# The first token tile's gate and up products spread over the last set of the cross attention

## The chip, the cores and the metric

The kernel runs on one core of one Trainium2 chip, as a single launch. The metric is device time in microseconds (us) of an execution. TensorE (PE, with its weight loads as PEld) does the matrix products, VectorE (DVE), ScalarE (ACT) and GpSimd (POOL) the elementwise work, and SyncE (SP) issues most of the DMAs.

## The reference

A pre-norm decoder layer in float32 over x of (4, 512, 512) tokens, with a context of (4, 1024, 512):

```python
x = x + _L0_attn_ref(_layernorm(x), ...)      # sliding-window self attention, grouped output
x = x + _L0_xattn_ref(_layernorm(x), ctx, ctx, mask, ...)   # 16 heads, 4 key groups, ALiBi
x = x + _L0_ffn_ref(_layernorm(x), w_gate, w_up, w_down)
```

The change touches the seam between the second and the third line. The cross attention is `softmax(Q K^T / sqrt(32) + slope * rel) V`, then a product with `Wo`. The feed-forward part quantizes its input per token to 8 bits and its weights to -1, 0, 1:

```python
gate = bitlinear(x, w_gate)                    # act_quant(x) @ weight_quant(w).T, 512 -> 2048
up = bitlinear(x, w_up)
intermediate = jax.nn.silu(gate) * up
return h_bitlinear(intermediate, w_down)       # Walsh-Hadamard transform over 2048, quantize, 2048 -> 512
```

## The kernel before

Three stages follow each other: the self attention, the cross attention, the feed-forward loop. The 2048 tokens are 16 token tiles of 128 rows.

**Cross attention.** The work is cut into `SETS` = 16 sets (4 batches times 4 heads of a group), and each set into 8 steps of 128 keys, 128 steps in all, 0 to 127. A step has, on TensorE in the order that is written in the code: row maxima of a set that lies ahead (L1085, 4 products into PSUM bank set "sm", each reduced by DVE, L1089), the score products (`scores`, L1145, two PSUM tiles `st` with two buffers), side work that a plan hangs on single steps (`extra`), the low-part products (`weights`, L1156), the exponentials on ACT (L1163, two of 128x1024 a step), and the weighted values of the step before (`weigh`, L1181). The exponentials are added up (L1170) by POOL, and in the last set by DVE, for the divisor (`divide`, L1195, copied by ACT at L1200). The row maxima run 10 steps ahead, so steps 118 to 127 have none. The last set is steps 120 to 127. Here only TensorE's order is fixed by hand; ACT, DVE and POOL are ordered by the scheduler.

**Tail of the cross attention.** After step 127: the last `weigh` and the last `divide`, four quotients (L1232, L1233) on DVE, the output products of the last two sets (`output`, L1240 on TensorE, added to the residual by DVE at L1245). Between them stand the gate and up products of the first token tile: `gated_mm(n)` makes 4 products for gate and 4 for up (L397, bf16, 128x512 each), then Silu on ACT (L402) out of PSUM; `gated_mul(n)` multiplies on DVE (L406); n is 0 to 3. `first(half)` is the first butterfly stage of the Walsh-Hadamard transform on DVE (L382, L383) from `mid` into `mix`.

**Feed-forward loop.** It runs s from 0 to 20 and works on five tiles at once: `now` is tile s, `prev` tile s-1, and so on. The order on TensorE, ACT and DVE is the written one. For `now`: `gated_mm`, `gated_mul`, `first`, and `turn(q)`, four transposes (L138) into one PSUM bank, copied by ACT (L139). For `prev`: the rest of the turns, `inner(q)`, four products with the 128x128 Hadamard matrix (L433), copied by ACT to `y` (L436), and the outer butterfly stages on DVE (`outer`, L382 and L383). For `old`: `sizes` (L445, absolute values on ACT), `peak` (L453 on DVE) and `quantize` (L326, L327 on ACT). Then the down product (L495). Two passes of the loop, s = 0 and s = 1, fill this pipe: at s = 0 only the first tile's `turn(0)` and `turn(1)` are done.

`mid` lies in the buffer "qs3" and `mix` in "qs2", one buffer each, both queries of cross-attention sets before. The gate weights are loaded at step 98 and the up weights at step 114. The rows of the tiles 12 and 13 are normalized in the loop (L92, L93 at s = 1).

Of the kernel before, what the change touches and what calls it, by code (L numbers as in the profile page):

```python
# [12 lines left out]
F32 = mybir.dt.float32  # L13
# [5 lines left out]
AF = mybir.ActivationFunctionType  # L19
ALU = mybir.AluOpType  # L20
# [3 lines left out]
P = 128  # L24
B, T, D = 4, 512, 512
NT = B * T // P
QT = T // P
DC = D // P
# [6 lines left out]
KT = KEYS // P  # L35
DH = 32
FF = 2048
FC = FF // P
# [15 lines left out]
def decoder_layer(  # L54
# [7 lines left out]
    nc = tc.nc  # L62
# [121 lines left out]
    def some_bank(shape, name):  # L184
        return bank["pool"].tile(shape, F32, tag=bank["tag"], name=name)
# [143 lines left out]
    xqTs, sgus = {}, {}  # L329
# [55 lines left out]
    class Tile:  # L385
# [23 lines left out]
            )  # L409

        def first(self, half):
            if half == 0:
                self.mix = bw.tile([P, FC, P], F32, tag="qs2", name="mix")
            butterfly(self.mid[:, ts(half, 8), :], self.mix[:, ts(half, 8), :], 0)
# [98 lines left out]
    with tc.tile_pool(name="aw", bufs=1) as aw, tc.tile_pool(name="akv", bufs=2) as akv, \  # L515
# [435 lines left out]
        with tc.manual_schedule(engines={mybir.EngineType.PE, mybir.EngineType.Activation}):  # L951
# [30 lines left out]
            for n in range(len(units) + 2):  # L982
                if n == len(units) - 3:
# [3 lines left out]
                    bx = late.enter_context(tc.tile_pool(name="bx", bufs=1, side="right"))  # L987
# [45 lines left out]
    bw = ctx.enter_context(tc.tile_pool(name="bw", bufs=1))  # L1033
    wT = {}

    def ternary_load(which):

        if which == "u":
            wT[which] = []
            for i in range(2):  # L1040
                w = bw.tile([P, DC // 2, FF], BF16, tag=f"qs{i}", name=f"w_u{i}")
                nc.sync.dma_start(out=w, in_=ternary[which][:, 2 * i:2 * i + 2, :])
                wT[which] += [w[:, 0], w[:, 1]]
        else:
            shape, tag = ([P, DC, FF], "ks0") if which == "g" else ([P, FC, D], "ks1")
            w = bw.tile(shape, BF16, tag=tag, name=f"w_{which}")
            for n in range(4):
                at = ts(n, shape[1] // 4)
                nc.sync.dma_start(out=w[:, at], in_=ternary[which][:, at])
            wT[which] = [w[:, c] for c in range(shape[1])]  # L1050

    with tc.tile_pool(name="b1", bufs=1) as b1, \
# [174 lines left out]
        def quotients(m):  # L1227
            nc.gpsimd.tensor_tensor(oTs[m], oTs[m], recs[m], ALU.mult)

        def quotient(m, qt):  # L1230
            rec, o = recs[m][:, ts(qt, P)], oTs[m][:, ts(qt, P)]
            nc.vector.reciprocal(rec, rec)  # L1232
            nc.vector.tensor_tensor(o, o, rec, ALU.mult)  # L1233
# [14 lines left out]


        SETS = B * HG  # L1250
        extra, at_end = {}, {}

        def plan(step, what, *args, to=extra):
            to.setdefault(step, []).append(lambda: what(*args))
# [82 lines left out]
                plan(step + 3 + i, side_rows, pair, to=at_end)  # L1337
        plan(KT * HG * 3 + 2, lambda: ternary_load("g"))
        plan(KT * HG * 3 + 18, lambda: ternary_load("u"))

        with tc.manual_schedule(engines={mybir.EngineType.PE}):
            nms[0] = small.tile([P, G, QT, 2], F32, tag="nm2", name="nm2", bufs=2)
            first.values(0)
            first.turn(2, nc.scalar)
            first.keys(2)
            first.values(1)
            first.turn(3)
            first.keys(3)  # L1350
            first.send(1)
            for i in range(G * QT):
                row_maxima(0, i)
                if i in (2, 4):
                    side_queries(1, i // 4)
                if i in (6, 8):
                    first.values(i // 2 - 1)
                if i == 8:
                    batches[1] = KeysValues(1)
                    batches[1].rows()  # L1360
            merge(0)
            last = None
            for step in range(-2, KT * SETS):
                m, kt = divmod(step, KT)
                now = 0 <= step < KT * SETS
                ahead, i0 = divmod(step + 10, KT)
                maxima = [
                    lambda i=i: row_max(ahead, 4 * i0 + i) for i in range(4)
                ] if 0 <= ahead < SETS else []
                for f in maxima[:2]:  # L1370
                    f()
                sts = [scores(m, kt, 0)] if now else None
                for f in maxima[2:3]:
                    f()
                if now:
                    sts.append(scores(m, kt, 1))
                for f in maxima[3:]:
                    f()
                for f in extra.pop(step, []):
                    f()  # L1380
                if maxima and i0 == KT - 1:
                    merge(ahead)
                ps = weights(m, kt, sts) if now else None
                if last is not None:
                    weigh(*divmod(step - 1, KT), last)
                if kt == 1 and 1 <= m < SETS:
                    divide(m - 1, before_last)
                    spread(m - 1)
                if kt == 2 and 1 <= m < SETS:
                    reciprocals(m - 1)  # L1390
                if kt == 4 and 1 <= m < SETS:
                    quotients(m - 1)
                for f in at_end.pop(step, []):
                    f()
                before_last, last = last, ps
            ternary_load("d")
            weigh(SETS - 1, KT - 1, last)
            divide(SETS - 1, last)
            scores_pool.close()
            gup = ctx.enter_context(tc.tile_pool(name="cgu", bufs=4, space=PSUM, side="right"))  # L1400
            tiles = [Tile(t) for t in range(NT)]
            tiles[0].gated_mm(0)
            tiles[0].gated_mm(1)
            for qt in range(QT):
                quotient(SETS - 1, qt)
            for n in range(2):
                tiles[0].gated_mul(n)
                tiles[0].gated_mm(n + 2)
                output(SETS - 2, (2 * n, 2 * n + 1), 2)
            for n in range(2, 4):  # L1410
                tiles[0].gated_mul(n)
            for half in range(2):
                tiles[0].first(half)
        assert not extra and not at_end
        late.close()


# [2 lines left out]
    with tc.tile_pool(name="c1", bufs=1) as c1, \  # L1420
            tc.tile_pool(name="c2", bufs=2) as c2, \
            tc.tile_pool(name="ctr", bufs=1, space=PSUM) as ctr, \
            tc.tile_pool(name="cdp", bufs=1, space=PSUM) as cdp, \
            tc.tile_pool(name="cmm", bufs=2, space=PSUM) as cmm, \
            tc.manual_schedule(
                engines={mybir.EngineType.PE, mybir.EngineType.DVE, mybir.EngineType.Activation}
            ):
        had = c1.tile([P, P], F32, name="had")
        nc.scalar.dma_start(out=had, in_=c_had)
        class Nothing:  # L1430
            def __getattr__(self, name):
                return lambda *args: None

        def tile_at(t):
            return tiles[t] if 0 <= t < NT else Nothing()

        last_xqT = c1.tile([P, QT, DC, P], BF16, name="xqT")
        last_rows = [
            ffn_rows(NT - 4 + i, 2, c1, ("h3", "xq"), (1, 1), lambda i0, i=i: last_xqT[:, i:i + 2])
            for i in (0, 2)  # L1440
        ]
        bank.update(pool=cmm, tag="mm")
        for s in range(NT + 5):
            now, prev, old, older, oldest = (tile_at(s - d) for d in range(5))
            if s == 0:
                now.turn(0)
                now.turn(1)
                continue
            older.back(0)
            old.sizes(0)  # L1450
            old.outer(3)
            if s <= NT:
                oldest.result()
            prev.inner(0)
            now.gated_mm(0)
            old.sizes(1)
            older.back(1)
            prev.inner(1)
            old.peak()
            if s > NT:  # L1460
                oldest.result()
            prev.turn(2)
            now.gated_mm(1)
            prev.turn(3)
            now.gated_mul(0)
            prev.inner(2)
            prev.inner(3)
            now.gated_mul(1)
            now.first(0)
            old.quantize(0)  # L1470
            if 1 <= s < 13:
                next(last_rows[(s - 1) // 6], None)
            now.gated_mm(2)
            now.turn(0)
            prev.outer(1)
            old.quantize(1)
            now.gated_mul(2)
            now.gated_mm(3)
            prev.outer(2)
            now.gated_mul(3)  # L1480
            now.first(1)
            older.down()
            now.turn(1)
# [53 lines left out]
```

## Time and profile before

| | us |
|---|---|
| median of 3 runs | 1608.52 |
| lowest, highest | 1608.39, 1610.01 |
| the profiled execution's own time | 1607.11 |
| its span | 1605.0 |
| TensorE busy in the span | 1553.0 |
| DVE busy | 1166.0 |
| ACT busy | 894.2 |
| POOL busy | 807.2 |

The profile is one execution of the program. Its span runs from the first to the last instruction; the execution's own time has 2.11 us more around it. A row of a timeline gives the start in the span, the time from the first instruction's start to the last one's end, the engine, the line of the code, the operation, output and inputs, and how many instructions were merged; in brackets stands the idle time of the engine before it and what released it. The end of a matmul is modelled, and matmuls overlap, so a run of four 128x512 products shows 1.03 us where the next run begins 0.865 us after it. A few matmul records are missing.

### The profile page before, as it was taken

Reading aid. Unit: us, or ns where it says so; the run is one execution under the profiler, and the core shown is the slowest. Engines: PE = TensorE matmul, PEld = TensorE weight load, DVE = VectorE, ACT = ScalarE, POOL = GpSimd, SP = SyncE. Lnnn points to the kernel's source line nnn. Section 1 sums busy time; section 2 is a strip of 40 time slices with the busy share of each in tenths; the row PEclk is TensorE's granted clock in tenths of the full one; section 3 lists DMA queues with packets and bytes.
Section 4 is the critical chain, followed back from the end, with each engine's and each line's share of the span. In section 5 each row is a group of like instructions: output and inputs, shape, how many; then the busy total and the mean of one; then the engine's idle time right before and its main releaser. Section 6 shows DMA issues by size and latency. Waiting matters only on the chain.

```text
span 1605.0 us, 23009 instructions
## 1 busy us (share of the span) xinstructions
PE 1553.0 (97%) x7826; PEld 911.6 (57%) x7856; DVE 1166.0 (73%) x2249; ACT 894.2 (56%) x1870; POOL 807.2 (50%) x558
## 2 busy tenths in 40 slices
PE   7999999999999999799999999999999999999997
PEld 4566666556655665555555555555544435666664
DVE  4676897998888862565666666665677657999987
ACT  1454555455455562145544454445575765988886
POOL 2433343354444431368888888888789930011010
PEclk9999999999999999799999999999999999999999
DMA  8522222233223201421212111121122110222121
GB/s 269 157 99 79 79 79 68 74 92 89 75 85 88 68 1 37 103 65 42 61 28 65 50 51 38 46 71 25 42 84 58 36 61 8 45 48 48 48 53 46
DMA packets 127317, 106.90 MB, mean 67 GB/s; under 512 B 81268, under 2 KB 88568, under 8 KB 126776
## 3 DMA queue, kind: packets, MB, share of 16 engines
q1 hardware_dynamic: 118896, 90.85, 20.9%
q10 hardware_dynamic: 7152, 13.44, 2.6%
q0 software_dynamic: 1152, 1.15, 0.3%
q8 instruction: 62, 1.02, 0.3%
q14 instruction: 55, 0.45, 0.1%
HBM read 61.75 MB, written 10.86 MB: 45 GB/s over the span
## 4 chain that ended last, share of the span: by engine, by line
PE 84%; DVE 7%; ACT 3%; issue 2%; DMA 1%; SPq 1%; POOL 0%; DVEq 0%; ACTq 0%; POOLq 0%
PE y L701 14%; PE s_ps L1085 8%; PE st L1145 7%; PE o_ps L1181 7%; PE sc L834 4%; PE xo_ps L1240 3%; PE q_ps L810 3%; PE q_ps L297 3%; PE av L894 3%; PE st L1156 3%; PE f_ps L689 3%; PE y_ps L433 2%; PE g_ps L397 2%; PE u_ps L397 2%; PE d_ps L495 2%; PE tr_ps L138 2%
## 5 line engine op out<-in xcount | busy, mean ns | idle before, releaser
L1170 POOL TENSOR_TENSOR sum<-sum,p 128x1024 f32<-128x1024 f32 x180 | 423.1, 2384 | 19.0 <-ACT p L1163 18.9
L1089 DVE TENSOR_REDUCE nm<-s_ps 128x1 f32<-128x512 f32 x480 | 300.9, 683 | 140.1 <-PE s_ps L1085 139.6
L1163 ACT ACTIVATE p<-st 128x1024 f32<-128x1024 f32 x256 | 248.0, 1020 | 96.8 <-PE st L1156 92.8
L701 PE MATMUL y<-wf,attnT 128*128 128x512 f32 x512 | 251.7, 602 | 0.0
L861 POOL TENSOR_TENSOR p<-p,den 128x512 f32<-128x512 f32 x64 | 67.9, 1060 | 260.4 <-DVE den L860 198.7
L1085 PE MATMUL s_ps<-ks,qs 99*128 99x512 f32 x480 | 186.4, 429 | 1.6 <-DVE nm L1089 0.6
L1145 PE MATMUL st<-qs,ks 101*128 101x512 f32 x512 | 166.4, 406 | 7.3 <-ACT p L1163 5.5
L1085 PEld LDWEIGHTS s_ps<-ks,qs 99*128 99x128 f32 x480 | 81.9, 190 | 111.5 <-issue 25.4
L1181 PE MATMUL o_ps<-p,va 128*32 128x512 f32 x1024 | 136.9, 605 | 0.0
L504 POOL TENSOR_TENSOR res<-res,xres 128x512 f32<-128x512 f32 x13 | 23.7, 1826 | 198.2 <-ACT res L503 198.2
L701 PEld LDWEIGHTS y<-wf,attnT 128*128 128x128 f32 x512 | 86.1, 190 | 59.8 <-issue 59.1
L1170 POOL TENSOR_TENSOR sum<-p,p 128x1024 f32<-128x1024 f32 x30 | 70.7, 2377 | 97.2 <-ACT p L1163 76.8
L1145 PEld LDWEIGHTS st<-qs,ks 101*128 101x128 f32 x512 | 87.8, 189 | 54.2 <-ACT p L1163 40.7
L853 ACT ACTIVATE p<-s,nm 128x128 f32<-128x128 f32 x256 | 99.5, 392 | 14.0 <-DVE nm L845 13.9
L85 POOL TENSOR_TENSOR rs<-ss,neghalf 128x4 f32<-128x4 f32 (+1 forms) x72 | 79.0, 1097 | 54.3 <-DVE ss L595 50.8
L825 ACT COPY qT<-qtr 128x512 f32<-128x512 f32 x64 | 37.5, 586 | 109.6 <-PE qtr L823 109.6
L908 ACT COPY attnT<-av 128x256 f32<-128x256 f32 x128 | 42.8, 375 | 78.5 <-PE av L900 71.7
L834 PEld LDWEIGHTS sc<-kT,qT 128*128 128x128 f32 x512 | 73.0, 190 | 18.3 <-issue 15.1
L397 PEld LDWEIGHTS <-xqT 128*128 128x128 bf16 x512 | 50.0, 98 | 47.8 <-issue 1.4
L834 PE MATMUL sc<-kT,qT 128*128 128x160 f32 (+4 forms) x512 | 76.9, 293 | 0.0
L816 POOL TENSOR_TENSOR q<-q,rs 128x512 f32<-128x512 f32 x64 | 66.6, 1041 | 7.4 <-DVE q L592 2.6
L810 PE MATMUL q_ps<-wqu_sb,qcT 128*128 128x512 f32 x128 | 66.3, 599 | 0.6 <-DVE ss L595 0.6
(214 smaller groups left out, 3078.3 us busy)
## 6 DMA issues: line engine op xcount, KB each, us to landing
qs<-qH SPq DMA_DIRECT2D x128, 64.0 KB, 2.0
cx<-in_ctx SPq DMA_DIRECT2D x30, 256.0 KB, 2.8
w<-in_L_attn_out_w SPq DMA_DIRECT2D x16, 256.0 KB
w<-in_L_attn_out_w SPq DMA_DIRECT2D x4, 1024.0 KB
raw<-in_L_ffn_w_gate SPq DMA_DIRECT2D x4, 1024.0 KB, 5.1
raw<-in_L_ffn_w_up SPq DMA_DIRECT2D x4, 1024.0 KB
raw<-in_L_ffn_w_down SPq DMA_DIRECT2D x4, 1024.0 KB, 5.1
raw<-in_L_ffn_w_gate ACTq DMA_DIRECT2D x8, 512.0 KB, 4.1
```

Of the source, the lines that this page charges most:

```text
L85: nc.gpsimd.tensor_tensor(dst, src, neghalf[:, :src.shape[1]], ALU.pow)
L397: nc.tensor.matmul(acc, lhsT=xqTs[self.t][:, c, :], rhs=w[c][:, ts(n, 512)], start=(c == 0), stop=(c == DC - 1),)
L701: nc.tensor.matmul(y, lhsT=attnT[:, h, :], rhs=wf[:, h, :], start=(h == 0), stop=(h == HEADS - 1))
L810: nc.tensor.matmul(q_ps, lhsT=made[self.b][0][:, ts(self.qt, P)], rhs=wqu_sb[:, ts(self.g, HG * P)], start=True, stop=True,)
L834: nc.tensor.matmul(sc[:, j, lo:hi], lhsT=self.qT[:, j].rearrange("p h r -> p (h r)"), rhs=kT[:, (qt - 1) * P + lo:(qt - 1) * P + hi], star ...
L853: nc.scalar.activation(self.p[:, j, :], s[:, j, :], AF.Exp, bias=nm[:, j:j + 1], accum_out=den[:, j:j + 1],)
L1085: nc.tensor.matmul(s_ps, lhsT=qss[hh][0:R_TOP, g, ts(qt, P)], rhs=kss[b % 2][0:R_TOP, g, ts(hf, T)], start=True, stop=True,)
L1089: nc.vector.tensor_reduce(nms[m][:, g, qt, hf:hf + 1], s_ps, AX.X, ALU.max, negate=True)
L1145: nc.tensor.matmul(st[:, g % 2, :], lhsT=ks[0:R_TOP + 2, g, ts(kt, P)], rhs=qss[hh][0:R_TOP + 2, g, :], start=True, stop=False,)
L1163: nc.scalar.activation(p, st, AF.Exp)
L1170: by.tensor_tensor(sums[m][i], last[i] if kt == 1 else sums[m][i], ps[i], ALU.add)
L1181: nc.tensor.matmul(accs[m][at, :], lhsT=va[:, kt, at], rhs=ps[g // 2][:, g % 2, :], start=(kt == 0), stop=(kt == KT - 1),)
```

## The change

The first token tile's products leave the tail. `raw(n, which)` makes one group of four products (gate for even, up for odd steps) in each of the steps 120 to 127, ahead of the score products, into a PSUM bank of the set "sm", and DVE copies it unscaled to SBUF: gate to the buffer "h2T", up to "qs2". `gated_raw(half)` then makes Silu (on ACT, in place) and the multiplication (on DVE) out of SBUF, each on half a tile, 128x1024. In the tail the second tile's `gated_mm` and `gated_mul` stand where the first one's stood. In the loop the pass s = 1 has no gate and up products, and from s = 2 on each pass has those of tile s, as before.

```diff
+        def raw(self, n, which):
+            if n == 0:
+                pool, tag = (bx, "h2T") if which == "g" else (bw, "qs2")
+                setattr(self, which, pool.tile([P, FC, P], F32, tag=tag, name="raw"))
+            ps = some_bank([P, 4, P], "raw_ps")
+            for c in range(DC):
+                nc.tensor.matmul(
+                    ps, lhsT=xqTs[self.t][:, c, :], rhs=wT[which][c][:, ts(n, 512)],
+                    start=(c == 0), stop=(c == DC - 1),
+                )
+            nc.vector.tensor_copy(getattr(self, which)[:, 4 * n:4 * n + 4, :], ps)
+
+        def gated_raw(self, half):
+            g, u = (z[:, ts(half, 8), :] for z in (self.g, self.u))
+            nc.scalar.activation(g, g, AF.Silu, scale=sgus[self.t][:, 0:1])
+            nc.vector.scalar_tensor_tensor(g, u, sgus[self.t][:, 1:2], g, ALU.mult, ALU.mult)
+            self.mid = self.g
...
+        tiles = [Tile(t) for t in range(NT)]
+        for n in range(KT):
+            plan(KT * (SETS - 1) + n, tiles[0].raw, n // 2, "gu"[n % 2], to=at_start)
...
-                for f in maxima[:2]:
+                for f in maxima[:2] + at_start.pop(step, []):
                     f()
                 sts = [scores(m, kt, 0)] if now else None
...
-            tiles = [Tile(t) for t in range(NT)]
-            tiles[0].gated_mm(0)
-            tiles[0].gated_mm(1)
+            tiles[1].gated_mm(0)
+            tiles[1].gated_mm(1)
             for qt in range(QT):
                 quotient(SETS - 1, qt)
+            for half in range(2):
+                tiles[0].gated_raw(half)
             for n in range(2):
-                tiles[0].gated_mul(n)
-                tiles[0].gated_mm(n + 2)
+                tiles[1].gated_mul(n)
+                tiles[1].gated_mm(n + 2)
                 output(SETS - 2, (2 * n, 2 * n + 1), 2)
-            for n in range(2, 4):
-                tiles[0].gated_mul(n)
             for half in range(2):
                 tiles[0].first(half)
+            for n in range(2, 4):
+                tiles[1].gated_mul(n)
...
+            gates = tile_at(s if s > 1 else -1)
...
-            now.gated_mm(0)
+            gates.gated_mm(0)
```

All `gated_mm` and `gated_mul` calls of the loop go to `gates` in the same way; `tile_at(-1)` is an object whose calls do nothing.

In the changed kernel the new lines are L420 (products of `raw`), L424 (its copy), L428 (Silu) and L429 (multiplication of `gated_raw`), and lines behind them stand 19 higher or more.

More of the change, by code (lines that the diff above doesn't have):

```diff
@@ L1250, in decoder_layer @@
         SETS = B * HG
-        extra, at_end = {}, {}
+        extra, at_end, at_start = {}, {}, {}
         def plan(step, what, *args, to=extra):
@@ L1400, in decoder_layer @@
             gup = ctx.enter_context(tc.tile_pool(name="cgu", bufs=4, space=PSUM, side="right"))
-            tiles = [Tile(t) for t in range(NT)]
-            tiles[0].gated_mm(0)
-            tiles[0].gated_mm(1)
+            tiles[1].gated_mm(0)
+            tiles[1].gated_mm(1)
             for qt in range(QT):
                 quotient(SETS - 1, qt)
+            for half in range(2):
+                tiles[0].gated_raw(half)
             for n in range(2):
-                tiles[0].gated_mul(n)
-                tiles[0].gated_mm(n + 2)
+                tiles[1].gated_mul(n)
+                tiles[1].gated_mm(n + 2)
                 output(SETS - 2, (2 * n, 2 * n + 1), 2)
-            for n in range(2, 4):
-                tiles[0].gated_mul(n)
             for half in range(2):
                 tiles[0].first(half)
-        assert not extra and not at_end
+            for n in range(2, 4):
+                tiles[1].gated_mul(n)
+        assert not extra and not at_end and not at_start
         late.close()
@@ L1462, in decoder_layer @@
             prev.turn(2)
-            now.gated_mm(1)
+            gates.gated_mm(1)
             prev.turn(3)
-            now.gated_mul(0)
+            gates.gated_mul(0)
             prev.inner(2)
             prev.inner(3)
-            now.gated_mul(1)
+            gates.gated_mul(1)
             now.first(0)
@@ L1472, in decoder_layer @@
                 next(last_rows[(s - 1) // 6], None)
-            now.gated_mm(2)
+            gates.gated_mm(2)
             now.turn(0)
@@ L1476, in decoder_layer @@
             old.quantize(1)
-            now.gated_mul(2)
-            now.gated_mm(3)
+            gates.gated_mul(2)
+            gates.gated_mm(3)
             prev.outer(2)
-            now.gated_mul(3)
+            gates.gated_mul(3)
             now.first(1)
```

## The prediction

> **What bounds it now.** I read the page's engine totals first, then the busy time by stretches around the change, then the timelines of TensorE, ACT and DVE in the last set, its tail and the first two passes of the feed-forward loop. 0.2% of the median, 3.2 us, is about what a measurement of this kernel can tell from no change.
>
> The page, then the stretches (columns: stretch, length, busy time of PE, PEld, DVE, ACT and POOL, granted clock, DMA share, GB/s): last set, tail, loop passes 0 and 1, pass 2, most of the rest.
>
> ```profile
> PE 1553.0 (97%) x7826; PEld 911.6 (57%) x7856; DVE 1166.0 (73%) x2249; ACT 894.2 (56%) x1870; POOL 807.2 (50%) x558
> ```
> ```profile
> 1287.20:1317.90 30.70, 28.35 (x168) 9.77 (x160) 16.91 (x16) 20.48 (x24) 10.80 (x6) 1.00 0.08 19
> 1317.90:1335.30 17.40, 16.62 (x71) 7.06 (x68) 11.96 (x20) 5.97 (x8) 0.00 (x0) 1.00 0.29 106
> 1335.30:1349.50 14.20, 13.36 (x86) 9.61 (x89) 6.76 (x12) 7.93 (x13) 1.82 (x2) 1.00 0.02 6
> 1349.50:1365.50 16.00, 13.16 (x81) 8.52 (x81) 14.61 (x22) 12.72 (x21) 0.00 (x0) 1.00 0.09 17
> 1365.50:1580.00 214.50, 209.84 (x1262) 136.09 (x1284) 200.81 (x279) 187.93 (x278) 25.62 (x15) 1.00 0.22 49
> ```
> TensorE looks full everywhere, but a matmul counts as busy to its modelled end. One plain step of the last set on TensorE, then ACT in set and tail (start, us, engine, line):
>
> ```profile
> 1305.73 0.50 PE L1156 MATMUL st<-qL,kL 32*128 32x512 f32 x4
> 1306.16 1.06 PE L1181 MATMUL o_ps<-p,va 128*32 128x512 f32 x8
> 1307.41 0.73 PE L1145 MATMUL st<-qs,ks 101*128 101x512 f32 x2 [0.18 <-ACT p L1163]
> 1308.32 0.73 PE L1145 MATMUL st<-qs,ks 101*128 101x512 f32 x2 [0.18 <-ACT p L1163]
> 1308.99 0.50 PE L1156 MATMUL st<-qL,kL 32*128 32x512 f32 x4
> ```
> ```profile
> 1312.73 1.94 ACT L1163 ACTIVATE p<-st 128x1024 f32<-128x1024 f32 x2 [1.26 <-PE st L1156]
> 1315.93 1.94 ACT L1163 ACTIVATE p<-st 128x1024 f32<-128x1024 f32 x2 [1.26 <-PE st L1156]
> ...
> 1320.74 0.59 ACT L1200 COPY rec<-den 128x512 f32<-128x512 f32 x1 [1.13 <-PE den L1195]
> 1321.74 1.28 ACT L402 ACT_TABLE_LOAD   x1 [0.42 <-PE g_ps L397]
> 1323.04 1.27 ACT L402 ACTIVATE sl<-g_ps,sgu_all 128x512 f32<-128x512 f32 x2
> ```
> The step is a ring: scores wait for the exponentials of the step before (they free PSUM), exponentials wait for the scores. It turns in 3.20 us, and ACT idles 1.26 of it. In the tail the two TensorE groups of L397 start 0.865 us apart, 0.216 a matmul.
>
> **The change, part by part.** The instruction order of the built programs shows what the diff does not. ACT and DVE are ordered by the scheduler there, and it lifts the first tile's Silu into the set: half 0 between the exponentials of steps 122 and 123, half 1 between those of 126 and 127, each with a table load before it and one back to Exp behind it. The order on SP and POOL is the same, and no DMA is added or passed.
>
> Product groups (+1.4). Eight groups of 0.865 us go ahead of the scores. In a plain step TensorE is free 0.72 after the exponentials start (two L1181 passes of 0.445 from 1306.16, against the exponential at 1306.33), and 0.82 with the 0.1 that a change from 32-column to full-array work adds (last den pass 1320.09, next group 1320.62, pass 0.43). The group ends at 1.68. The scores then need 1.10 to the L1156 row, as in the crowded step 122 (1298.18 to 1299.28): 2.78 where it was 2.66, and with the drain of the last weigh pass the TensorE ring is 3.38 against 3.20. That is +0.18 in steps 125 and 126. Steps 120 and 121 come 0.3 later, but there the divisor matmuls wait for POOL's last sum (L1170, five sums of 2.37 us ending 1296.71), which leaves 0.13. Step 122 has no hole, so its group costs 0.9. Steps 123, 124 and 127 run theirs while ACT stands at the Silu. Sum 0.13 + 0.9 + 0.36 = 1.4. Bounds: 0 if the holes take all, 8 x 0.865 = 6.9 if none does; I stay near the plain step's rows, which show the hole.
>
> Silu in the set (+4.9). Each half is queued ahead of the next two exponentials, and the whole ring waits behind. From first exponential to first exponential: 1.94 (two exponentials) + 1.28 (load) + 1.15 (Silu of 128x1024 from SBUF with a per-row scale, by the L326 row of that shape, 1154 ns) + 1.28 = 5.65, against 3.20. The Exp load waits for TensorE's scores, which are there by then. So 2.45 each, 4.9 for both. The copies that Silu reads (L424, 0.69 by the L139 DVE copy of that shape) are done in time: DVE's step is 2.36 of sums + 0.69, under 3.2. Unknown is what a load costs directly behind a running ACT instruction: here the load began 0.42 after ACT had stopped, so 0 to 0.42 could hide per load, 0 to 1.7 for four. I take 0, since the Silu starts 0.02 after the load ends.
>
> [...]
>
> Tail (0). TensorE does the same 32 products, now the second tile's, the same output matmuls, back to back. DVE gains the half-1 multiply (1.3) and keeps four first-butterfly halves (4 x 0.68), now queued ahead of the reciprocals. Counted from Silu's end, about 1321.0 in shifted time, they finish near 1325.1, and the divisor copy that the reciprocals need comes near 1327.6: covered by 2.5 us, and up to that lost if Silu is late.
>
> Loop (-3.7). Pass 1 loses 32 products (6.9 us of TensorE), four Silus and four multiplies. What is late next is the short chain through one transpose bank: transpose, ACT copy, transpose, 1.33 us a turn. Its rows, and the DVE chain behind it:
>
> ```profile
> 1335.36 0.66 PE L138 MATMUL tr_ps<-ident,mix 128*128 128x128 f32 x4 [0.78 <-DVE xres L1245]
> 1336.05 0.59 ACT L139 COPY mT<-tr_ps 128x512 f32<-128x512 f32 x1 [5.05 <-PE tr_ps L138]
> 1336.69 0.66 PE L138 MATMUL tr_ps<-ident,mix 128*128 128x128 f32 x4 [0.68 <-ACT mT L139]
> 1337.18 1.06 PE L433 MATMUL y_ps<-had,mT 128*128 128x128 f32 x8
> ```
> ```profile
> 1347.08 1.23 DVE L382 TENSOR_TENSOR y<-y 128x1024 f32<-128x1024 f32 x1 [0.19 <-ACT sl L402]
> ...
> 1351.15 1.22 DVE L383 TENSOR_TENSOR y<-y 128x1024 f32<-128x1024 f32 x1
> ```
> ```profile
> 1352.40 1.06 ACT L445 ACTIVATE ab<-y 128x1024 f32<-128x1024 f32 x1 [2.05 <-DVE y L383]
> ```
> Count from the first transpose, 1335.36. Transposes at 0 and 1.33, inner products 1.82 and 2.72 (0.9 each), third transpose 3.62, its ACT copy behind two y copies 4.32 to 4.91, fourth transpose 4.96, done 5.56. That frees mix: the second tile's butterfly half 5.65 to 6.87 (two of 0.61), the row statistics of 1.7 to 8.57, 0.19 of waits, then two outer stages of 4.55 without the 0.74 of L406 between them: 13.3. Before, the same stages ended at 1352.37, 17.0. The next ACT work (L445) waits for exactly this, and behind it the y and mT copies and the transposes of pass 2, so the lead is 3.7 there. TensorE has no backlog (13.16 of 16.0 busy in pass 2), and from 1365.5 on both kernels run the same order. Bounds: the two multiplies alone, 1.4, to all of TensorE's 6.9.
>
> Sum: 1.4 + 4.9 + 0 - 3.7 = **+2.6 us**. On the profiled execution, span 1605.0 of 1607.11, that is 1607.6 of 1609.7; on the median of 1608.52, which lies 1.4 above it, 1611.1.
>
> **Rivals.**
> Dearer switches, slower: ACT empties before each added load. Place: the four loads in the set; price up to 0.42 each, +1.7, sum +4.3, 1612.8. It decides from 0.15 a load, since 3.2 - 2.6 = 0.6. For it: loads now follow directly on a running instruction, which the trace never shows. Against: Silu starts 0.02 behind its load.
> TensorE counts, about equal: the loop is 97.8% TensorE-busy from 1365.5, and if that, not the copy chain, decides, all 6.9 come back: 1.4 + 4.9 - 6.9 = -0.6, 1607.9. Against: the idle 2.05 ahead of L445.
> Cheap set, faster: ACT's 1.26 of idle and the ring's slack hide the Silu pairs wholly, and the loop returns 6.9: 1.4 - 6.9 = -5.5, 1603.0. Against: 3.71 of inserted work does not fit into 1.26.
>
> **How the numbers follow.** The forecast has 0.50; its own spread, 1609.1 to 1612.5 (loop 3.0 to 5.2, Silu pairs 2.2 to 2.8 each), crosses the line at 1611.7, with 0.37 below and 0.13 above. Dearer switches 0.35, all slower. TensorE counts 0.10, within 0.2%. Cheap set 0.05. So faster 0.05, same 0.47, slower 0.48. The range runs from the second rival, 1607.9, rounded to 1607.5, to 1616.0, near the dear bound of the product groups (2.6 + 5.5 above the median is 1616.6).
>
> **What would show it.** Five more ACT_TABLE_LOAD rows would be wrong: I expect four more, at two places 16 us apart, with 5.65 between the exponentials' starts there and about 3.4 in steps 125 and 126; the set's last exponential 6.3 later than 1315.93; 17.4 of tail kept; L445 of the first tile 13.3 after the first transpose, not 17.0. Loads with idle time ahead of them mean the first rival. If the groups cost 0.865 in plain steps too, or the tail grows by the butterflies, I am wrong upwards; if pass 2 starts over 5 us earlier and keeps it, downwards.

## The result and the profile after

The changed kernel takes **1612.34 us** (median of 11 runs, 1610.79 to 1614.04), against 1608.52 of the kernel before, run beside it on the same chip (11 runs, 1608.08 to 1610.06). The ratio is 1.0022, with a 95% interval from 1.0013 to 1.0031: slower by 3.8 us (2.1 to 5.0 by the interval), where 2.6 was forecast. The profiled execution took 1612.17, of which the span is 1610.36. The span before was 1604.98, so the two traces are 5.38 apart.

The engine totals of the page after:

```profile
PE 1557.0 (97%) x7856; PEld 914.0 (57%) x7856; DVE 1170.9 (73%) x2255; ACT 898.9 (56%) x1872; POOL 806.8 (50%) x558
```

TensorE issues what it did before (x7856 weight loads in both). ACT has two instructions more: four table loads and two Silus of 128x1024 came, four Silus of 128x512 went. TensorE's busy time is 4.0 higher for the same products, but 30 matmul records are missing before, so the two totals can't be compared closely, and the busy time by stretches is read instead. The columns are those of the prediction: after the length and the five busy times comes the granted clock. The first five rows are the last set, the tail, passes 0 and 1 of the loop, pass 2, and most of the rest; the sixth is a cut out of set and tail:

```profile
1288.74:1326.38 37.64, 33.91 (x204) 13.59 (x200) 26.00 (x30) 28.85 (x30) 11.30 (x6) 0.99 0.15 49
1326.38:1344.56 18.18, 17.40 (x68) 6.92 (x61) 9.71 (x16) 5.10 (x8) 0.00 (x0) 0.93 0.08 33
1344.56:1354.40 9.84, 7.70 (x62) 6.97 (x63) 3.90 (x7) 5.48 (x10) 1.09 (x2) 1.00 0.03 8
1354.40:1370.60 16.20, 12.04 (x72) 7.46 (x70) 14.02 (x21) 11.70 (x20) 0.72 (x1) 1.00 0.09 17
1370.60:1585.40 214.80, 211.51 (x1288) 136.51 (x1288) 202.46 (x280) 188.56 (x279) 24.83 (x15) 1.00 0.22 49
...
1325.40:1328.80 3.40, 3.40 (x18) 0.98 (x18) 0.68 (x2) 1.57 (x3) 0.00 (x0) 0.50 0.71 276
```

Read the clock column. Every stretch of the kernel before around the change had 1.00. Here the tail has 0.93, and the last row shows why: for 3.4 us TensorE was granted half its clock.

The set is next, on ACT (start, time, line; two exponentials a step):

```profile
1302.24 1.94 ACT L1182 ACTIVATE p<-st 128x1024 f32<-128x1024 f32 x2 [0.24 <-PE st L1175]
1304.20 1.28 ACT L428 ACT_TABLE_LOAD   x1
1305.50 1.15 ACT L428 ACTIVATE raw<-raw,sgu_all 128x1024 f32<-128x1024 f32 x1
1306.66 1.28 ACT L1182 ACT_TABLE_LOAD   x1
1307.96 1.94 ACT L1182 ACTIVATE p<-st 128x1024 f32<-128x1024 f32 x2
...
1319.78 1.28 ACT L428 ACT_TABLE_LOAD   x1
1321.08 1.15 ACT L428 ACTIVATE raw<-raw,sgu_all 128x1024 f32<-128x1024 f32 x1
1322.24 1.28 ACT L1182 ACT_TABLE_LOAD   x1
1323.54 1.94 ACT L1182 ACTIVATE p<-st 128x1024 f32<-128x1024 f32 x2
```

The four loads are at the two places forecast, 15.6 us apart. The exponentials of step 123 start 5.71 after those of step 122 (1307.96 and 1302.24, each rounded), and those of step 127 come 5.71 after those of step 126. No row after the first has a bracket: ACT never waits there, and each load starts 0.01 or 0.02 after the instruction before it ends.

TensorE meanwhile waits for ACT, in the first row for step 124's scores, in the second for step 127's weighted values:

```profile
1309.03 0.73 PE L1164 MATMUL st<-qs,ks 101*128 101x512 f32 x2 [1.58 <-ACT p L1182]
...
1324.62 1.98 PE L1200 MATMUL o_ps<-p,va 128*32 128x512 f32 x6 [1.97 <-ACT p L1182]
```

The second wait, of 1.97, is followed by the half clock: it begins at 1325.4, 0.8 after the wait ends.

The loop, with the first tile's transposes, second butterfly half, outer stages and the ACT work that waits for them (L464 is the line that was L445):

```profile
1344.56 0.65 PE L138 MATMUL tr_ps<-ident,mix 128*128 128x128 f32 x4 [0.79 <-DVE xres L1264]
1349.55 0.66 PE L138 MATMUL tr_ps<-ident,mix 128*128 128x128 f32 x4 [0.73 <-ACT mT L139]
1350.24 0.69 DVE L382 TENSOR_TENSOR mix<-mid 128x512 f32<-128x512 f32 x1 [5.73 <-PE tr_ps L138]
1356.88 1.22 DVE L383 TENSOR_TENSOR y<-y 128x1024 f32<-128x1024 f32 x1
1358.13 1.06 ACT L464 ACTIVATE ab<-y 128x1024 f32<-128x1024 f32 x1 [3.54 <-DVE y L383]
```

Counted from the first transpose, the fourth comes at 4.99 (forecast 4.96), the butterfly half at 5.68 (5.65), L464 at 13.57 (13.3).

The two executions, cut at the same instructions:

| stretch | before | after | difference |
|---|---|---|---|
| start to step 119's exponentials | 1287.20 | 1288.74 | +1.54 |
| to step 127's exponentials (the set) | 28.73 | 34.80 | +6.07 |
| to the loop's first transpose (the tail) | 19.42 | 21.02 | +1.59 |
| to the first tile's peak (L453 before, L472 after) | 21.19 | 16.93 | -4.26 |
| to the second tile's peak | 15.46 | 16.25 | +0.79 |
| the rest | | | -0.35 |
| span | 1604.98 | 1610.36 | +5.38 |

The first row lies ahead of anything that the change touches. That point comes between 1287.20 and 1290.38 in the twelve records of all kernels here, and the record before is the earliest, so the row is left out as scatter. The other rows sum to +3.84. That the medians differ by 3.82 is closer than their interval, 2.1 to 5.0, lets one expect: the two records are one execution each.

### The profile page after: what moved, and what is told of

Its sections match the earlier page's. It is cut to its first block, busy times and chain, and to the rows that moved or that the text cites. A ratio compares the mean times of both kernels' runs of the same rounds, so it can differ in the third digit from the quotient of the medians.

```text
span 1610.4 us, 23040 instructions
## 1 busy us (share of the span) xinstructions
PE 1557.0 (97%) x7856; PEld 914.0 (57%) x7856; DVE 1170.9 (73%) x2255; ACT 898.9 (56%) x1872; POOL 806.8 (50%) x558
## 4 chain that ended last, share of the span: by engine, by line
PE 85%; DVE 7%; ACT 4%; issue 2%; DMA 1%; SPq 1%; POOL 0%; DVEq 0%; ACTq 0%; POOLq 0%
PE y L720 13%; PE s_ps L1104 8%; PE st L1164 7%; PE o_ps L1200 7%; PE sc L853 4%; PE xo_ps L1259 3%; PE q_ps L297 3%; PE f_ps L708 3%; PE q_ps L829 3%; PE av L913 3%; PE st L1175 3%; PE y_ps L452 3%; PE d_ps L514 2%; PE tr_ps L138 2%; PE g_ps L397 2%; PE u_ps L397 2%
## 5 line engine op out<-in xcount | busy, mean ns | idle before, releaser
L383 DVE TENSOR_TENSOR y<-y 128x1024 f32<-128x1024 f32 x48 | 67.1, 1399 | 0.0
```

## The experiments

The main theory is the prediction's sum, now with a fifth term: two switches at 2.5 each in the ring, some 1 us of groups, the half clock of 1.6, and the loop's -3.7 or so. The rivals are its own: dearer loads, and a loop that TensorE's 6.9 decides.

**The products alone** (`raw_only`). The kernel before, with the eight groups and DVE's copies added; nothing reads them, and there is no Silu on them.

```diff
+        for n in range(KT):
+            plan(KT * (SETS - 1) + n, tiles[0].raw, n // 2, "gu"[n % 2], to=at_start)
```

> The kernel before with the eight product groups and their copies in steps 120 to 127 added, their results unused; tail and loop as before. Theory 1: 0.7 us in step 122, 0.1 in each other plain step, together 1.35: 1609.9 us. Rival (groups dominate): 0.865 us in each of eight steps, 1613 to 1615 us.

Measured: 1608.79 (11 runs, 1607.40 to 1611.85) against 1608.47, ratio 1.0002 [0.9993, 1.0011]. In the trace the set is 30.05 long against 28.73: +1.32 where 1.4 was worked out. The rings of the steps 123 to 127 are 3.28, 3.37, 3.27, 3.33 and 3.35 against 3.19, 3.26 and three times 3.20, so a group that finds a hole costs 0.07 to 0.15 there; step 122, which has none, costs 0.6. The time shows less, 0.3 with an interval of 1.4 on either side, and can't tell 1.3 from nothing.

**The switches alone** (`switch_only`). The kernel before, with two Silus of 128x1024 on a constant tile, each queued behind the exponentials where the changed kernel has it; no products are added and the loop is kept.

```diff
+            with tc.issue_after(scratch['exp']):
+                nc.scalar.activation(z, z, AF.Silu, scale=sgus[0][:, 0:1])
```

> The kernel before, with only the two Silus of 128x1024 and their four table loads put between the exponentials of steps 122 and 123 and of 126 and 127, on a constant tile that nothing reads. Theory 1: each pair turns 3.2 us between the exponentials' starts into 5.7, together 5.0 us; with the half clock in the tail up to 1.6 more: 1613.5 to 1615.1 us. Rival (ACT's 1.26 us of idle hides most of it): under 1611 us.

Measured: 1615.47 (5 runs, 1613.76 to 1616.13), ratio 1.0040 [1.0026, 1.0053], +7.0, just above the range expected. The rings at the two Silus are 5.71, as in the changed kernel, so two switches cost 5.0. The rest is again a half clock, and a long one. It begins at 1308.1, 1.85 us after the exponentials that TensorE waits for behind the first Silu pair (they start at 1306.25); that wait is some 2.7 us by estimate, the 0.18 of a plain step and the 2.51 by which this ring is longer. The stretch between the first switch and the second:

```profile
1308.10:1318.30 10.20, 10.06 (x34) 3.82 (x34) 6.29 (x6) 4.47 (x6) 1.77 (x1) 0.50 0.01 4
```

Three steps lie in it, with rings of 4.04, 4.54 and 4.23 for 3.2: another 3.2 us. The switch is no dearer than 2.5; what follows it is.

**The loop alone** (`loop_only`). The kernel before, without the gate and up products in pass 1.

```diff
+            gates = tile_at(s if s > 1 else -1)
+            if s == 1:
+                now.mid = prev.mid
...
-            now.gated_mm(0)
+            gates.gated_mm(0)
```

> The kernel before, with pass 1 of the loop left without gate and up products (the second tile transforms the first tile's values instead of its own). Theory 1: 3.5 to 3.8 us faster, 1604.9 us, the first tile's outer stages end 13.5 us after the first transpose instead of 17.0. Rival (the loop is paced by TensorE's count): 6.9 us faster, 1601.6 us.

Measured: 1604.46 (11 runs, 1602.26 to 1607.87), ratio 0.9976 [0.9967, 0.9986], -4.0. TensorE loses all of the 6.9 of products here, and 4.0 comes back: the copy chain decides, not TensorE's sum. In this trace the first transpose is at 1337.26, and what waits for the outer stages starts 13.57 later, the same as in the changed kernel, still waiting for DVE:

```profile
1350.83 1.06 ACT L445 ACTIVATE ab<-y 128x1024 f32<-128x1024 f32 x1 [3.53 <-DVE y L383]
```

This kernel has no Silu in the set, and its record is at half clock for 3.4 us all the same, in pass 2 of the loop. TensorE waits there for the ACT copy of a transpose, 2.12 us in this record and 2.13 in the first record of the changed kernel, against 1.59 in the kernel before. The wait and the stretch here, and the same wait in the changed kernel, whose first record stays at 1.00 behind it:

```profile
1363.47 1.11 PE L138 MATMUL tr_ps<-ident,mix 128*128 128x128 f32 x4 [2.12 <-ACT mT L139]
```
```profile
1363.40:1366.80 3.40, 3.33 (x14) 2.86 (x15) 3.24 (x4) 3.37 (x6) 0.00 (x0) 0.50 0.01 2
```
```profile
1370.77 0.66 PE L138 MATMUL tr_ps<-ident,mix 128*128 128x128 f32 x4 [2.13 <-ACT mT L139]
```

**The Silus moved behind the tail's** (`late_silu`, and once more as `late_again`). The changed kernel, with the two halves ordered behind the second tile's last Silu that stands ahead of them, where the table is already loaded.

```diff
-            for half in range(2):
-                tiles[0].gated_raw(half)
+            with tc.issue_after(tiles[1].last_sl):
+                for half in range(2):
+                    tiles[0].gated_raw(half)
```

> The changed kernel with one edit: the first tile's two Silus are queued on ACT behind the second tile's second Silu in the tail, so the last set has no table load. Theory 1 (the four loads and two Silus in the set cost 5.0 us and lead to a TensorE wait that halves its clock): the set's last exponentials 1.35 us later than before, not 6.1; no half clock in the tail; the loop still 3.6 earlier; time 1608.5 + 1.35 - 3.6 = 1606.3 us, faster than the kernel before. Rival (the product groups on TensorE are what the set pays for): the set stays 4 to 6 us longer, 1609 to 1611 us.

> The kernel with the late Silus once more, since its first runs lay in two groups. Theory 1 (set 1.35 later, loop 3.5 earlier): 1606.4 us, ratio 0.9987. Rival (something in the tail or loop that the profile does not show eats it): 1608.6 us again.

Measured: 1608.63 (11 runs, 1604.88 to 1612.06), ratio 0.9995 [0.9985, 1.0005], a miss; the second time 1607.30 (11 runs, 1603.51 to 1610.23), ratio 0.9988 [0.9978, 0.9998], where 0.9987 was expected. The two intervals overlap. The traces agree with the account: the set is 30.08 and 30.10 long, the tail 19.43, the loop as in the changed kernel. The runs themselves are scattered: the first time four with a mean granted clock of 0.993 take 1604.9 to 1606.3, three with 0.988 to 0.990 take 1609.7 to 1612.1. So the moved Silus give back the two switches and the 1.6 that followed their waits. That the slower runs lose it again to half clocks elsewhere fits their lower mean clocks, but only one run of each eleven has a trace, so it is not shown.

**Is the half clock the wait's?** TensorE was given unused products to fill the wait of step 127 (`after_busy`), and the changed kernel was run twice more, unaltered (`after_again`, `after_third`).

```diff
+            for c in range(8):
+                nc.tensor.matmul(
+                    busy, lhsT=xqTs[0][:, c % DC, :], rhs=wT["g"][c % DC][:, 0:512],
+                    start=(c == 0), stop=(c == 7),
+                )
```

> The changed kernel with eight products more (1.73 us of TensorE, result unused) ahead of the last weigh of step 127, where TensorE waited 1.97 us for the second Silu pair. Theory (that wait halves TensorE's clock for the tail): the set's rings unchanged at 5.7 us, no half clock between 1320 and 1345, tail from the last exponentials to the first transpose 19.4 instead of 21.0; time 1612.3 - 1.6 = 1610.7 us. Rival (the half clock fell there by chance): 1612.3 us as the changed kernel, and the half clock in other places as often.

> The changed kernel once more, for a second profile. Theory (the wait in step 127 causes the half clock): again a half clock that begins 1 to 4 us after the second Silu, and a tail of about 21.0 us. Rival (chance): a tail of 19.4 and the half clock elsewhere.

> The changed kernel a third time, for a third profile. As for the second: a tail of 21.0 us by the theory that the wait causes it, 19.4 us by the rival that it is chance.

`after_busy` took 1612.45 (7 runs, 1611.24 to 1614.59), ratio 1.0024 [1.0013, 1.0035]: its tail is back at 19.43, with a granted clock of 1.00 from 1290 to 1345, but the time is not better; its record has 3.4 us at 0.51 from 1370.1 on, in the loop. The unaltered kernel took 1612.75 and 1612.08, and both times its tail is 19.42 too. In `after_again` the half clock lies elsewhere, behind the *first* wait. The wait and the stretch:

```profile
1308.43 0.73 PE L1164 MATMUL st<-qs,ks 101*128 101x512 f32 x2 [1.58 <-ACT p L1182]
```
```profile
1310.20:1313.60 3.40, 3.40 (x15) 0.64 (x14) 2.38 (x3) 1.94 (x2) 1.63 (x1) 0.51 0.00 0
```

Step 125's ring is 4.73 there instead of 3.27, step 124's 0.12 longer and step 126's 0.04 shorter: 1.54 together, about as much as the tail lost in the first profile. No DMA runs in this stretch (the last two numbers), so the 276 GB/s in the stretch of the first profile are not what it takes. The theory that step 127's wait alone brings it falls. What holds in both of these profiles of the changed kernel is this: one stretch of 3.4 us, at 0.50 or 0.51, follows one of the two waits, and costs 1.5 to 1.6.

**Both waits filled** (`both_busy`). As before it, with six more unused products ahead of step 124's scores.

```diff
+        plan(KT * (SETS - 1) + 4, fill_wait, 6, to=at_start)
...
+            fill_wait(8)
```

> The changed kernel with TensorE kept busy in both Silu waits: six products (1.3 us) ahead of step 124's scores and eight (1.73 us) ahead of the last weigh, results unused. Theory (each Silu wait can drop TensorE to half clock, and in a given execution one of the two does): the rings stay 5.7 us, no half clock between 1295 and 1345, the other steps 3.3 to 3.4 and the tail 19.4; time 1.5 us under the changed kernel, 1610.8 us. Rival (the half clocks there come by chance): 1612.4 us and one in that stretch as before.

Measured: 1611.81 (11 runs, 1608.98 to 1613.50) against 1608.57, ratio 1.0018 [1.0009, 1.0026]. The second filler, the rest of the second wait, and the whole of set and tail:

```profile
1322.37 1.89 PE L1366 MATMUL busy<-w_g,xqT 128*128 128x512 bf16 x8
1324.48 1.54 PE L1200 MATMUL o_ps<-p,va 128*32 128x512 f32 x6 [0.22 <-ACT p L1182]
```
```profile
1288.64:1342.83 54.19, 52.72 (x283) 21.36 (x275) 35.71 (x46) 33.95 (x37) 11.28 (x6) 1.00 0.13 45
```

TensorE's waits have shrunk to 0.29 and 0.22, the clock is 1.00 from the set to the loop, and set and tail are 1.6 shorter than in the changed kernel (54.19 against 55.82), with the same switches. So the half clock there goes with TensorE's waits, as far as two profiles at 1.00, this one and that of `after_busy`, can show it. The time gained only 0.5, within the intervals. The mean granted clock of this execution is 0.990, where the first profile of the changed kernel has 0.991 with the half clock in its tail; so by estimate from the two means this one loses at least as much clock, outside set and tail.

The clock of two records, the kernel before and the first profile of the changed kernel, says more. In the changed kernel it falls to 0.50 at 649.54, 673.43, 724.63, 1325.38 and 1608.68 and is back at 1.00 at 656.36, 687.08, 728.04 and 1328.79; in the kernel before it falls at 648.91, 672.80 and 1604.64 and is back at 655.73 and 686.46. In each record all these times lie whole multiples of 3.413 us apart, as on the marks of a grid. Step 119's exponentials start 0.91 after a mark in the one, and on a mark in the other.

In the changed kernel's record the set's second wait, of 1.97, lies whole between two marks, 1321.96 and 1325.38, and at the latter the half clock begins. The first wait, of 1.58, is cut by the mark at 1308.31, the 2.13 in pass 2 by the one at 1369.75, and a wait of 2.34 that ends at 1586.52 by the one at 1584.79; the clock stays at 1.00 behind these three. In the kernel before a wait of 2.34 that ends at 1581.12 is cut into 1.97 and 0.37, and the clock stays at 1.00 too. But whole or cut does not decide either: in the kernel before, the wait of 1.59 in pass 2 lies whole, with 1.00 behind it; a wait of 1.42 ahead of 723.8 lies whole in both records, with 0.50 from 724.63 on in the changed kernel's and 1.00 in the other; and in the changed kernel's a wait of 2.11 that ends at 647.88 is cut, with 0.50 from the next mark, 649.54, on. What decides is not shown.

What remains is that each execution has its half clocks at its own places: set and tail are 1.6 shorter in `both_busy`, but from the first transpose to the end it takes 267.7 us, where the first profile of the changed kernel takes 265.8, with no half clock ahead of the record's last 2 us. Whether the fillers make half clocks later in the kernel more frequent stays open.

**A better order** (`spread`). `late_silu`, with the groups away from steps 122 and 127: gates in 118, 119, 125 and 126, ups in 120, 121, 123 and 124.

```diff
+        for n, (g, u) in enumerate(((-2, 0), (-1, 1), (5, 3), (6, 4))):
+            plan(KT * (SETS - 1) + g, tiles[0].raw, n, "g", to=at_start)
+            plan(KT * (SETS - 1) + u, tiles[0].raw, n, "u", to=at_start)
```

> The kernel with the late Silus, its product groups moved: gate groups in steps 118, 119, 125 and 126, up groups in 120, 121, 123 and 124, so none in the crowded step 122. Theory 1: step 122 gets its 0.62 us back, the other steps cost 0.1 each: 0.8 us for the groups, 3.5 to 3.8 from the loop, 1605.6 us, faster than the kernel before by 0.17%. Rival (the groups cost by count, wherever they stand): as with the late Silus alone.

Measured: **1605.74** (11 runs, 1603.15 to 1606.48) against 1608.70, ratio 0.9978 [0.9969, 0.9987]. It beats both kernels. Its interval overlaps that of `late_again`, so the gain over the late Silus alone is less sure. From the start of set 14 to step 127's exponentials it takes 60.77, against 60.36 before and 61.70 in `late_silu`: the eight groups cost 0.4 in all in this record. Its Silus follow one table load in the tail:

```profile
1323.01 1.28 ACT L402 ACT_TABLE_LOAD   x1 [0.42 <-PE g_ps L397]
1324.30 1.27 ACT L402 ACTIVATE sl<-g_ps,sgu_all 128x512 f32<-128x512 f32 x2
1325.46 2.18 ACT L430 ACTIVATE raw<-raw,sgu_all 128x1024 f32<-128x1024 f32 x2
```

## Why the prediction was right, and where it was not

**Product groups, +1.4.** Right: 1.32 alone (`raw_only`), 1.04 in the changed kernel, where the groups of steps 123, 124 and 127 add nothing behind the Silus, as the prediction had it. The step without a hole cost 0.68 of the 0.9. Steps 125 and 126 turn in 3.27 and 3.35 where "about 3.4" was expected. `spread` shows that the price was one of place: 0.4.

**Silu in the set, +4.9.** Right: 2 x 2.51. The ring is 5.71 instead of 5.65, because the four instructions are 0.02 apart each. The set's last exponential is 6.07 later than before, counted from step 119, against 6.3.

**Dearer switches.** Wrong as a mechanism, although its 1612.8 is nearest to the time. It asked for up to 0.42 hidden in each load; no load in the set has idle time ahead of it, and the rings at the Silus are 5.71 or 5.72 in the first profile of the changed kernel and in `switch_only`. The two switches there and back cost 5.02 with everything.

**Tail, 0.** This is the term that failed. The prediction looked for a late Silu, and for butterflies that outgrow their cover of 2.5. DVE's butterflies did not: they are done 4.5 before its reciprocals start. What was missed is what TensorE does after it has waited. The sum counted ACT's 2.45 at each switch as the whole price, and never asked what the wait, seen from TensorE, brings behind it. It brought 1.59 in the tail of the first profile, or 1.54 in steps 124 to 126 of another. With this term the first profile's sum is 5.0 + 1.0 + 1.6 - 3.8 = 3.8. The size of this term in the medians is less sure than in the profiles: filling both waits gave back 0.5, not 1.6, and the interval of the median, 2.1 to 5.0, holds the forecast's 2.6 as well.

That the time fell inside the forecast's own spread, 1609.1 to 1612.5, is in part luck. The 1.6 that was missing is partly offset by groups that cost 0.4 less than their term, and the spread was wide enough for the rest on account of the loop and the Silu pairs, which came within 0.2 of theirs.

**Loop, -3.7.** Right: -3.82 in the first profile, -4.0 in `loop_only`. It did not see that the shorter loop lengthens a TensorE wait in pass 2 from 1.59 to 2.12 or 2.13, with 3.4 us at a granted clock of 0.50 behind it in `loop_only`, while the clock stays at 1.00 in the first profile of the changed kernel. The rival that TensorE counts (-6.9) falls with `loop_only`, and *cheap set* with the two rings of 5.71.

## What to carry to other kernels

Where a scheduler orders an engine, find out where it puts an activation that needs another table set: the diff showed the Silus in the tail, where the table was loaded anyway, and the scheduler put them into a ring that waits for ACT, at two loads of 1.28 each. Put added products only into steps where TensorE has a hole; the same eight groups cost 1.3 in one place and 0.4 in another. When an engine is made to wait, ask what it does once it runs again, not only how long it stood.

## What the runs showed of the hardware

A wait of TensorE of 1.58 or 1.97 us was followed by 3.4 us at a granted clock of 0.50 or 0.51 in two profiles of the changed kernel: the 1.97 in the first, from 1325.4 on, the 1.58 in `after_again`, from 1310.2 on, and in neither behind both. In `switch_only`, where the first ring with a Silu takes 5.71, 10.2 us at 0.50 followed, from 1308.1 on. The kernel before and `spread`, without those waits, had 1.00 in set and tail.

The length of a wait alone does not decide. TensorE's wait in pass 2 of the changed loop had 3.4 us at 0.50 behind it in `loop_only`, where it is 2.12 long, and 1.00 in the first profile of the changed kernel, where it is 2.13; a wait of 2.34 near the end of the loop had 1.00 behind it in that profile and in the kernel before. All changes of the clock in these two records lie whole multiples of 3.413 us apart. The same kernel had its half clock at 1325.4 in one execution and at 1310.2 in another.
